# Block transposes that read with a stride, value rows in natural order, and fewer heads on VectorE at the border of two graphs

## The chip, the cores and the metric

The kernel runs on one core of one Trainium2 chip. The core has TensorE (PE: matmuls, and weight loads on a row of their own, PEld), VectorE (DVE), ScalarE (ACT), GpSimd (POOL) and SyncE (SP, which here only issues DMAs). They run at the same time and wait for each other through semaphores. The metric is the device time of one execution in microseconds (us); lower is better.

## The reference

There are 16 graphs of 1024 nodes with 256 features each, and an adjacency matrix per graph in which about one entry in 32 is set, the diagonal included. Two layers follow each other. Layer 0 normalizes the rows, applies a ReLU, and does masked attention with 8 heads of 32 features:

```python
h = jnp.maximum(_layernorm(x, axis=-1), 0.0)
Q, K, V = (proj(Wq, bq), proj(Wk, bk), proj(Wv, bv))          # per head
scores = jnp.einsum('bhnd,bhmd->bhnm', Q, K) * SCALE
scores = jnp.where(adj[:, None] == 0, -jnp.inf, scores)
attn = jax.nn.softmax(scores, axis=-1)
out = jnp.einsum('bhnm,bhmd->bhnd', attn, V)                  # heads joined
x = x + jnp.einsum('bno,po->bnp', out, Wo) + bo
```

Layer 1 normalizes again and attends once more, with one set of scores per kind of edge:

```python
h = jnp.maximum(_layernorm(x, axis=-1), 0.0)
e_k = leaky_relu(einsum('bid,bjd->bij', h * a_k[:, 0], h), 0.2)   # k = 0..3
scores = where(adj == k + 1, e_k, -9e15)
x = x + einsum('bij,bjd->bid', softmax(scores), h)
```

With the inputs given, entries of the adjacency are 0 or 1, so only the first kind occurs.

## The kernel before

**Tiles and steps.** A tile is 128 rows of one graph; a graph has 8 tiles, and 128 tiles are done in one loop (`for s in range(B * NT + 1)`), each with an inner loop over the 8 heads. Several pieces of work of different tiles run in one step of the loop: `now` is the tile whose layer 0 scores are made, `was` the one before it, whose heads are finished; `piece` and `piece_was` are rows of the next graph that are normalized and projected into queries, keys and values nine tiles ahead; `edge` and `edge_was` are tiles of layer 1, nine tiles behind. Each engine works in the order in which the loop issues; nothing reorders it. A tile's DMAs go on two queues, SP's and POOL's, and each is worked off in the order of its issues.

**A head.** TensorE makes a head's scores, 128x1024, in two matmuls (`scores`, L455) into one of two PSUM places, `sides[h in (4, 6)]`: heads 4 and 6, and layer 1's scores, use the second place, all others the first. VectorE adds the mask and takes the row minimum of the negated scores in one instruction (`softmax_max`, L467), which writes p to SBUF and so frees the PSUM place. ScalarE applies the exponential in place (`softmax_exp`, L475). Then p has to be turned, so that the 1024 keys lie on the partitions, and multiplied with the values (`combine`, L510; heads 0 to 3 at h = 7, heads 4 to 7 at h = 3 of the next tile).

**Two ways to turn.** For heads 2, 3, 6 and 7, TensorE makes eight 128x128 transposes and ScalarE copies them in two instructions (`turn`, `turn_half`, L574 and L575). For the heads in `BY_BLOCKS`, 0, 1, 4 and 5, VectorE transposes 32x32 blocks in one instruction (`blocks_of`, L376), and four DMAs on SP's queue place the four groups of partitions (`placed`, L381). The transpose reads p in one contiguous run. The keys therefore land on the partitions in another order within each 128: key 32b + k at partition 4k + b. The loop turns head h - 2 at head h, so head 5 of tile 7 is turned at h = 7 of that tile, and head 0 of tile 0 at h = 2 of that tile.

**Values.** Since two orders of keys exist, the values exist in two orders of rows: `values` (L339) makes columns 0 to 127 of v from `hTm`, whose rows are in the mixed order, and columns 128 to 255 from `hT`, in natural order. `place_of` tells where a head's 32 columns lie, the weight `wvT` and the bias `bv_t` have their columns in the same arrangement, and `combine` reads v at `place_of(h)`. The queries are made from `hTm` as well, so the tile's own rows are in mixed order in both layers. Layer 1 (`Edges`) uses `blocks_of` and `placed` too, on its own p, called sel.

**Keys.** A graph's eight keys are 512 KB loads from DRAM on SP's queue (`load_key`, L355). They replace the keys of the graph before in the same places, so they are issued at eight given steps (`KEY_STEPS`), four in tile 7 at h = 3, 4, 5 and 6, and four in tile 0 of the next graph at h = 0, 2, 3 and 4, between the block placements.

Of the kernel before, what the change touches and what calls it, by code (L numbers as in the profile page):

```python
# [17 lines left out]
P = 128  # L18
HEADS = 8
HD = 32  # L20
# [3 lines left out]
SLOPE = 0.2  # L24
NEG_INF = -9000000000000000.0
MASKED = -1e30
BY_BLOCKS = (0, 1, 4, 5)


def place_of(h):  # L30

    return (h // 2 % 2) * P + (h // 4) * 2 * HD + (h % 2) * HD


FLOOR = 1e28
# [7 lines left out]
def gnn_kernel(  # L43
# [18 lines left out]
    nc = tc.nc  # L62
    B, N, D = x.shape
    NT = N // P
    NC = D // P
    SCALE = HD ** (-0.5)
    HALF = 512
    NB = P // HD
# [35 lines left out]
    bv_t = const.tile([P, D], F32, name="bv_t")  # L104
    bo_t = const.tile([P, D], F32, name="bo_t")

    def load_biases():
        with nc.allow_non_contiguous_dma(reason="a few hundred elements, once"):
            nc.sync.dma_start(out=bq_t, in_=bq.rearrange("(c p) -> p c", p=P))
            nc.sync.dma_start(out=bk_t, in_=bk.rearrange("(c p) -> p c", p=P))  # L110
            for k, a in enumerate((a_0, a_1, a_2, a_3)):
                nc.sync.dma_start(out=a_t[:, :, k], in_=a.rearrange("(c p) o -> p (c o)", p=P))
        for i in range(2):
            nc.sync.dma_start(
                out=bv_t[:, i * P : (i + 1) * P].rearrange("p (r d) -> p r d", r=2),
                in_=bv.rearrange("(r i d) -> i r d", i=2, r=2)[i].partition_broadcast(P),
            )
        nc.sync.dma_start(out=bo_t, in_=bo.partition_broadcast(P))

    weight_rows = {}  # L120
# [6 lines left out]
    def transposed_weight(name):  # L127

        rows = weight_rows[name]
        wt = const.tile([P, NC, D], F32, name=name)  # L130
        tr = ps_tr.tile([P, 4, P], F32, tag="tr", name=f"{name}_tr")
        for fc in range(NC):
            for oc in range(NC):
                nc.tensor.transpose(tr[:, fc * NC + oc, :], rows[:, oc, fc * P : (fc + 1) * P], ident)
        if name == "wvT":
            for fc in range(NC):
                nc.vector.tensor_copy(
                    wt[:, fc].rearrange("p (i r d) -> p r i d", i=2, r=2),
                    tr[:, fc * NC : (fc + 1) * NC].rearrange("p r (i d) -> p r i d", i=2),
                )  # L140
        else:
            nc.vector.tensor_copy(wt.rearrange("p c f -> p (c f)"), tr.rearrange("p c f -> p (c f)"))
        return wt


    def norm_of(mv):

        g = nc.gpsimd
        n = mv.shape[1]

        def place(name, dtype=F32):
            if n <= 4:
                return small.tile([P, 4], dtype, tag=name, name=name)[:, :n]
            places.append(name)
            return many[:, len(places) * n - n : len(places) * n].bitcast(dtype)

        places = []
        if n > 4:
            many = work.tile([P, D], F32, tag="wide", name="many", bufs=1)

        ve = place("ve")
        g.tensor_scalar(ve, mv[:, :, 1], EPS, None, ALU.add)
        r = place("r")
        g.tensor_tensor(r, ve, less_half.to_broadcast([P, n]), ALU.pow)
        shift = place("shift")
        g.tensor_tensor(shift, mv[:, :, 0], r, ALU.mult)
        g.tensor_scalar(shift, shift, -1.0, None, ALU.mult)
        return r, shift
# [12 lines left out]
    qds, kds, vs, keysets, weights = {}, {}, {}, {}, {}  # L181

    class Piece:
# [146 lines left out]
        def values(self):  # L330
            b = self.b
            if b not in vs:
                vs[b] = graph.tile([P, NT, D], F32, tag="v", name=f"v_{b}")
            for t in range(self.n):
                ps = late if self.n == 1 else ps_tr.tile([P, D], F32, tag="tr", name="vproj")
                self.vproj = ps
                for i, hT in enumerate((self.hTm, self.hT)):
                    for fc in range(NC):
                        nc.tensor.matmul(  # L339
                            ps[:, i * P : (i + 1) * P],  # L340
                            lhsT=hT[:, fc, t * P : (t + 1) * P],
                            rhs=weights["wvT"][:, fc, i * P : (i + 1) * P],
                            start=(fc == 0),
                            stop=(fc == NC - 1),
                        )
                if self.n > 1:
                    self.biased(t)

# [25 lines left out]
    def blocks_of(p):  # L374
        blocks = work.tile([P, NB, NT, HD], F32, tag="blocks", bufs=3)
        nc.vector.transpose(blocks.rearrange("p b j q -> p j b q"), p)  # L376
        return blocks.rearrange("p b j q -> p b (j q)")
# [32 lines left out]
    class Attend:  # L410
# [69 lines left out]
            turn_half(self.probs[h][0], self.turned[h], half)  # L480

        def turn_blocks(self, h):
            self.blocks = blocks_of(self.probs[h][0])

        def place_blocks(self, h):
            self.turned[h] = placed(self.blocks, ptp.tile([P, N], F32, tag="pT", name="pT"))
# [19 lines left out]
        def combine(self, g):  # L506
            for j in range(NT):
                for r in range(GROUP):
                    h = g * GROUP + r
                    nc.tensor.matmul(  # L510
                        sums_place[r * HD : (r + 1) * HD, g * P : (g + 1) * P],
                        lhsT=vs[self.b][:, j, place_of(h) : place_of(h) + HD],
                        rhs=self.turned[h][:, j],
                        start=(j == 0),
                        stop=(j == NT - 1),
                    )
# [253 lines left out]
    with tc.manual_schedule():  # L770
# [6 lines left out]
        piece_was.load(nc.sync)  # L777
        now.load()
        load_biases()
        piece_next.load(nc.sync)  # L780
        mv = stats_place(NT)
# [3 lines left out]
        r, shift = norm_of(mv)  # L785
# [3 lines left out]
        for name in ("wkT", "wqT", "wvT", "woT"):  # L789
            weights[name] = transposed_weight(name)  # L790
# [28 lines left out]
        for s in range(B * NT + 1):  # L819
            b, t = divmod(s, NT)  # L820
# [8 lines left out]
            for h in range(HEADS):  # L829
                ending, eh = (now, h - 1) if h >= 1 else (was, HEADS - 1)  # L830
                turning, th = (now, h - 2) if h >= 2 else (was, HEADS + h - 2)
# [36 lines left out]
                if h == 3:  # L868
# [3 lines left out]
                        piece_was.biased()  # L872
                    if was:
                        was.combined()
                if turning and th in BY_BLOCKS:
                    turning.turn_blocks(th)
                    turning.place_blocks(th)
                elif turning:
                    turning.turn(th, 0)
                    turning.turn(th, 1)  # L880
# [162 lines left out]
```

## Time and profile before

| | us |
|---|---|
| runs: median (lowest to highest, three runs) | 3149.88 (3138.53 to 3151.07) |
| profiled execution: time | 3143.69 |
| its span, first to last instruction | 3141.9 |
| TensorE busy | 2941.3 (94%) |
| TensorE weight loads busy | 2202.9 (70%) |
| ScalarE busy | 2598.8 (83%) |
| VectorE busy | 2512.8 (80%) |
| POOL busy | 2172.4 (69%) |
| DMA packets of SP's queue, share of 16 engines | 54.5% |

The mean granted TensorE clock is 0.984 of full speed. VectorE does 520 block transposes of tiles called p (512 in layer 0 and 8 in the last graph's layer 1) and 120 of sel; both kinds take 1.24 us each. A line of groups reads: source line, engine, operation, out<-in by the program's names, partitions x elements and type, count, then busy us in all, mean ns of one, and after the last bar the idle time of the engine just before them with what ended it. In a timeline the first column is the start in us from the begin of the span, the second the length; in brackets stands the idle time before it. SPq is SP's queue of DMA issues. A window's row has, after the window, its length, the busy us of each engine with the number of instructions, the granted clock, the share of time that the DMA engines were busy, and GB/s.

### The profile page before, as it was taken

How to read it: one execution, taken by the hardware profiler on the slowest of the kernel's cores; microseconds unless marked ns; L12 is line 12 of the kernel's file. 1: busy time of each engine (PE TensorE's matmuls, PEld its weight loads, DVE VectorE, ACT ScalarE, POOL GpSimd, SP SyncE). 2: the span in 40 equal slices, each digit the busy share in tenths (PEclk: the TensorE clock that was granted, in tenths of full speed). 3: DMA queues.
4: the chain of work that ended last, by engine and by line, in shares of the span. 5: the costliest groups of instructions: out<-in, count | busy, mean ns of one | idle time of the engine just before them, and what ended most of it. 6: DMA issues, size and time to landing. Idle time of an engine off the chain costs nothing. (4 is left out here: it accounts for less than half of the span.)

```text
span 3141.9 us, 95789 instructions
## 1 busy us (share of the span) xinstructions
PE 2941.3 (94%) x36210; PEld 2202.9 (70%) x36210; DVE 2512.8 (80%) x4391; ACT 2598.8 (83%) x5157; POOL 2172.4 (69%) x2995
## 2 busy tenths in 40 slices
PE   5888999899999999999999999999999999998987
PEld 3666777677676777777777676777767777676663
DVE  4777888788787887878888787888878788787874
ACT  3888989889888988889889898888978888787871
POOL 2666777777777776777777777777767777675542
PEclk8999999999999999999999999999999999999999
DMA  6676787877878787787877878787787877777663
GB/s 214 208 245 212 230 272 220 270 217 230 255 229 263 223 263 225 226 268 223 270 227 235 251 234 257 228 258 229 234 261 215 271 223 227 245 232 239 185 174 96
DMA packets 634692, 729.22 MB, mean 232 GB/s; under 512 B 67376, under 2 KB 565424, under 8 KB 634224
## 3 DMA queue, kind: packets, MB, share of 16 engines
q1 hardware_dynamic: 565152, 510.86, 54.5%
q0 software_dynamic: 66960, 210.04, 20.5%
q8 instruction: 291, 4.77, 0.6%
q10 hardware_dynamic: 2112, 2.10, 0.2%
q14 instruction: 177, 1.45, 0.1%
HBM read 252.98 MB, written 134.22 MB: 123 GB/s over the span
## 5 line engine op out<-in xcount | busy, mean ns | idle before, releaser
L467 DVE CUSTOM_DVE_ANT_0 p<-s,neg 128x1024 f32<-128x1024 f32 x1024 | 1235.6, 1207 | 274.5 <-PE s L455 241.3
L475 ACT ACTIVATE p<-p,nmx 128x1024 f32<-128x1024 f32 x1024 | 1182.2, 1155 | 205.0 <-DVE nmx L467 202.5
L455 PE MATMUL s<-k,qt 128*128 128x512 f32 x2048 | 764.9, 455 | 107.9 <-DMA k<-kd 72.5
L376 DVE STREAM_TRANSPOSE blocks<-p 128x1024 f32<-128x1024 f32 x520 | 643.7, 1238 | 20.5 <-ACT p L663 10.6
L575 ACT COPY pT<-trp 128x512 f32<-128x512 f32 x1024 | 547.0, 590 | 106.2 <-PE trp L574 106.2
L510 PE MATMUL acc<-pT,v 128*32 128x128 f32 x16384 | 559.0, 281 | 37.1 <-DMA pT<-blocks 22.1
L510 PEld LDWEIGHTS acc<-pT,v 128*32 128x32 f32 x16384 | 472.6, 113 | 156.5 <-issue 82.9
L574 PE MATMUL trp<-ident,p 128*128 128x128 f32 x4096 | 531.2, 273 | 1.6 <-ACT pT L575 1.5
L574 PEld LDWEIGHTS trp<-ident,p 128*128 128x128 f32 x4096 | 478.1, 140 | 73.2 <-ACT pT L575 3.1
L435 POOL TENSOR_SCALAR neg<-adj 128x1024 bf16<-128x1024 int32 x128 | 467.6, 3653 | 79.5 <-ACT neg L447 70.2
L681 PE MATMUL acc<-h,pT 128*32 128x256 f32 x8192 | 494.7, 383 | 8.8 <-DVE ot L690 8.8
L455 PEld LDWEIGHTS s<-k,qt 128*128 128x128 f32 x2048 | 324.3, 192 | 215.5 <-issue 79.5
L681 PEld LDWEIGHTS acc<-h,pT 128*32 128x32 f32 x8192 | 241.8, 110 | 211.9 <-issue 63.8
L659 POOL TENSOR_TENSOR sel<-sel,less 128x1024 f32<-128x1024 f32 x120 | 286.6, 2388 | 64.9 <-ACT less L648 44.9
L616 PE MATMUL s<-h1T,ha 128*128 128x512 f32 (+2 forms) x744 | 272.8, 490 | 2.6 <-ACT h1T L553 1.3
L657 POOL TENSOR_SCALAR less<-top 128x1 f32<-128x1 f32 x120 | 31.6, 264 | 274.5 <-DVE top L639 274.5
L319 POOL DMA_DIRECT2D qd<-halves x240 | 177.0, 777 | 58.7 <-POOL halves L309 31.8
L494 POOL COPY wide<-rec 128x256 f32<-128x256 f32 x128 | 53.9, 421 | 226.5 <-DVE rec L492 226.5
L475 ACT ACTIVATION_READ_ACCUMULATOR p<-p,nmx 128x1 f32 x1024 | 202.7, 198 | 0.0
L325 POOL DMA_DIRECT2D kd<-halves x240 | 171.7, 764 | 35.4 <-POOL halves L309 35.4
L309 POOL TENSOR_TENSOR halves<-full,halves 128x256 fp32r<-128x256 f32 x240 | 176.3, 735 | 20.6
L648 ACT ACTIVATE less<-sel 128x1024 f32<-128x1024 f32 x120 | 127.0, 1058 | 65.6 <-DVE top L639 65.6
(120 smaller groups left out, 4238.8 us busy)
## 6 DMA issues: line engine op xcount, KB each, us to landing
pT<-blocks SPq DMA_DIRECT2D x2560, 128.0 KB, 3.6
k<-kd SPq DMA_DIRECT2D x128, 512.0 KB, 6.1
qt<-qd SPq DMA_DIRECT2D x128, 512.0 KB, 4.4
adj<-in_adj POOLq DMA_DIRECT2D x127, 512.0 KB, 5.1
qd<-halves POOLq DMA_DIRECT2D x240, 256.0 KB, 3.0
kd<-halves POOLq DMA_DIRECT2D x240, 128.0 KB, 4.0
xb<-in_x POOLq DMA_DIRECT2D x128, 128.0 KB, 4.4
x1d<-x SPq DMA_DIRECT2D x128, 128.0 KB, 4.0
```

Source lines behind the costliest of these rows:

```text
L319: nc.gpsimd.dma_start(out=qds[self.b][self.first, oc].rearrange("p u w n -> p u (w n)"), in_=halves.unsqueeze(1).to_broadcast([P, 2, 2 * P]),)
L376: nc.vector.transpose(blocks.rearrange("p b j q -> p j b q"), p)
L435: nc.gpsimd.tensor_scalar(self.neg, self.adj, 0.0, MASKED, ALU.is_equal, ALU.mult)
L455: nc.tensor.matmul(self.ps[:, cols], lhsT=self.qt[:, h, :], rhs=keysets[self.b][h][:, cols], start=True, stop=True,)
L467: nc.vector.tensor_tensor_reduce(out=p, in0=sides[h in (4, 6)], in1=self.neg, scale=-SCALE, scalar=FLOOR, op0=ALU.add, op1=ALU.min, accum_ ...
L475: nc.scalar.activation(p, p, AF.Exp, bias=nmx, scale=-1.0, accum_out=self.sums[:, h : h + 1])
L510: nc.tensor.matmul(sums_place[r * HD : (r + 1) * HD, g * P : (g + 1) * P], lhsT=vs[self.b][:, j, place_of(h) : place_of(h) + HD], rhs=self ...
L574: nc.tensor.transpose(tr[:, j, :], p[:, jj * P : (jj + 1) * P], ident)
L575: copy(pT[:, half * 4 : half * 4 + 4, :], tr)
L616: nc.tensor.matmul(self.side[:, cols], lhsT=self.ha[:, c, :], rhs=h1T[:, c, cols], start=(c == 0), stop=(c == NC - 1),)
L659: nc.gpsimd.tensor_tensor(self.sel, self.sel, self.less, ALU.subtract)
L681: nc.tensor.matmul(sums_place[a * HD : (a + 1) * HD, :], lhsT=self.pT[:, j, a], rhs=h1s[self.b][:, j, :], start=(j == 0), stop=(j == NT - 1),)
```

## The change

Values are kept in natural row order for all heads. The block transposes of layer 0 read p through a view that takes every fourth element, 32 of them, then the next offset, so that the natural order comes out on the partitions; the elements of one run of the read are 16 bytes apart. What the transpose writes and the four placing DMAs are the same. `values` then needs only `hT`, and makes all 256 columns in one pair of matmuls; `place_of` and the special arrangements of `wvT` and `bv_t` go. `hTm` stays, for the queries. Layer 1's own block transposes are not touched. As all heads read the same v, the set of heads that VectorE turns may differ by tile: it is 0, 1, 4 in tile 7, 1, 4, 5 in tile 0, and 0, 1, 4, 5 in the others.

```diff
-BY_BLOCKS = (0, 1, 4, 5)
-
-
-def place_of(h):
-
-    return (h // 2 % 2) * P + (h // 4) * 2 * HD + (h % 2) * HD
+BY_BLOCKS = {7: (0, 1, 4), 0: (1, 4, 5)}
+
+
+def by_blocks(t):
+    return BY_BLOCKS.get(t, (0, 1, 4, 5))
...
-        for i in range(2):
-            nc.sync.dma_start(
-                out=bv_t[:, i * P : (i + 1) * P].rearrange("p (r d) -> p r d", r=2),
-                in_=bv.rearrange("(r i d) -> i r d", i=2, r=2)[i].partition_broadcast(P),
-            )
+        nc.sync.dma_start(out=bv_t, in_=bv.partition_broadcast(P))
...
-        if name == "wvT":
-            for fc in range(NC):
-                nc.vector.tensor_copy(
-                    wt[:, fc].rearrange("p (i r d) -> p r i d", i=2, r=2),
-                    tr[:, fc * NC : (fc + 1) * NC].rearrange("p r (i d) -> p r i d", i=2),
-                )
-        else:
-            nc.vector.tensor_copy(wt.rearrange("p c f -> p (c f)"), tr.rearrange("p c f -> p (c f)"))
+        nc.vector.tensor_copy(wt.rearrange("p c f -> p (c f)"), tr.rearrange("p c f -> p (c f)"))
...
-                for i, hT in enumerate((self.hTm, self.hT)):
-                    for fc in range(NC):
-                        nc.tensor.matmul(
-                            ps[:, i * P : (i + 1) * P],
-                            lhsT=hT[:, fc, t * P : (t + 1) * P],
-                            rhs=weights["wvT"][:, fc, i * P : (i + 1) * P],
-                            start=(fc == 0),
-                            stop=(fc == NC - 1),
-                        )
+                for fc in range(NC):
+                    nc.tensor.matmul(
+                        ps,
+                        lhsT=self.hT[:, fc, t * P : (t + 1) * P],
+                        rhs=weights["wvT"][:, fc, :],
+                        start=(fc == 0),
+                        stop=(fc == NC - 1),
+                    )
...
-            self.blocks = blocks_of(self.probs[h][0])
+            self.blocks = blocks_of(self.probs[h][0].rearrange("p (j k b) -> p j b k", b=NB, k=HD))
...
-                        lhsT=vs[self.b][:, j, place_of(h) : place_of(h) + HD],
+                        lhsT=vs[self.b][:, j, h * HD : (h + 1) * HD],
...
-                if turning and th in BY_BLOCKS:
+                if turning and th in by_blocks(turning.t):
```

## The prediction

> **What bounds the kernel now.** I read first the page's busy shares, then the windows of single tiles, then the timeline of TensorE and VectorE where one tile passes into the next, then the groups of instructions for prices. The page names TensorE:
>
> ```profile
> PE 2941.3 (94%) x36210; PEld 2202.9 (70%) x36210; DVE 2512.8 (80%) x4391; ACT 2598.8 (83%) x5157; POOL 2172.4 (69%) x2995
> L376 DVE STREAM_TRANSPOSE blocks<-p 128x1024 f32<-128x1024 f32 x520 | 643.7, 1238 | 20.5 <-ACT p L663 10.6 <-DMA pT<-blocks 5.4 <-issue 2.5
> ```
>
> 94% is a mean over two kinds of tile. A tile is the time from one score reduction of head 0 (L467) to the next tile's. By their starts in the trace, tiles 1 to 6 of graphs 1 to 15 take 22.4 to 23.6 us on the mean of their place, 22.8 together; tile 7 takes 22.3; tile 0 takes 29.4. Tile 4 of graph 2 and tile 0 of graph 3 in the windows view (first column the window, then busy us by engine):
>
> ```profile
> 510.31:533.01 22.70, 22.65 (x287) 17.14 (x286) 19.45 (x34) 20.42 (x40) 18.82 (x29) 1.00 0.79 236
> 600.15:631.05 30.90, 23.57 (x287) 17.80 (x286) 19.64 (x34) 19.97 (x39) 20.59 (x29) 0.94 0.95 315
> ```
>
> In the ordinary tile TensorE is busy 22.65 of 22.70 us, and VectorE has 3.25 us to spare. In tile 0 both idle, and the DMA engines are at 0.95: TensorE waits for the next graph's keys, and its combine (L510) lasts 2.91 us where 1.95 is usual:
>
> ```profile
> 610.12 1.19 PE L455 MATMUL s<-k,qt 128*128 128x512 f32 x2 [3.62 <-DMA k<-kd]
> 611.24 2.91 PE L510 MATMUL acc<-pT,v 128*32 128x128 f32 x64
> ...
> 617.38 0.73 PE L455 MATMUL s<-k,qt 128*128 128x512 f32 x2 [0.83 <-DMA k<-kd]
> ...
> 627.67 0.70 PE L455 MATMUL s<-k,qt 128*128 128x512 f32 x2 [2.68 <-DMA k<-kd]
> ```
>
> VectorE's spare time is not spread evenly. At the seam between two ordinary tiles its timeline is
>
> ```profile
> 529.30 1.24 DVE L376 STREAM_TRANSPOSE blocks<-p 128x1024 f32<-128x1024 f32 x1
> 530.46 1.19 DVE L467 CUSTOM_DVE_ANT_0 p<-s,neg 128x1024 f32<-128x1024 f32 x1
> 531.58 0.08 DVE L467 DVE_READ_ACCUMULATOR2_ANT nmx<- 128x1 f32 x1
> 531.58 1.24 DVE L376 STREAM_TRANSPOSE blocks<-p 128x1024 f32<-128x1024 f32 x1
> 533.01 1.23 DVE L467 CUSTOM_DVE_ANT_0 p<-s,neg 128x1024 f32<-128x1024 f32 x1 [0.19 <-POOL shift L167]
> ```
>
> and TensorE's
>
> ```profile
> 532.15 0.73 PE L455 MATMUL s<-k,qt 128*128 128x512 f32 x2
> 532.72 1.04 PE L574 MATMUL trp<-ident,p 128*128 128x128 f32 x8
> 533.59 0.60 PE L610 MATMUL s<-ident,mirror 128*128 128x128 f32 x4
> 534.30 0.73 PE L455 MATMUL s<-k,qt 128*128 128x512 f32 x2
> ```
>
> Heads 0 and 1 share one PSUM place for scores, so TensorE's scores of head 1 (534.30) may start only when VectorE has reduced head 0 (533.01 + 1.23 = 534.24). That leaves 0.06 us of slack on TensorE and 0.19 us of idle on VectorE, behind the transposes of heads 4 and 5.
>
> **The change, part by part.** The sum is made against the profiled execution, 3143.7 us (span 3141.9), 6 us under the median of the runs, 3149.9.
>
> *v in natural order.* The value projection goes from eight TensorE instructions of 128 columns to four of 256. By the timeline the eight (L339) run from 516.33 until L500 starts at 517.22, 0.89 us. The output projection (L525) is the new form, four of 128x256: 521.84 until the next scores at 522.51, 0.67 us. So 0.22 us less in each of the 120 tiles that project, on TensorE where it is the bound. The eight projections of the start give 2 us, with one bias load and one weight copy fewer or simpler.
>
> *Fewer heads on VectorE in tiles 7 and 0.* 32 heads (5 of each tile 7, 0 of each tile 0) lose a 1.24 us block transpose and four SP DMAs of some 0.6 us of issue each, and gain eight TensorE transposes (532.72 to 533.59: 0.87 us) and two ScalarE copies (2 x 0.59 us; ScalarE idles over 2 us in every tile). Tile 7 is TensorE-bound: 0.87 - 0.22 = +0.65 us, 16 times, +10. In tile 0 the eight DMAs stand on SP ahead of the key loads:
>
> ```profile
> 602.26 5.46 SPq L381 DMA_DIRECT2D pT<-blocks  x4
> ...
> 611.95 4.12 SPq L381 DMA_DIRECT2D pT<-blocks  x4
> ```
>
> Those are head 5 of tile 7 and head 0 of tile 0. Landings of such DMAs on the full queue follow each other by some 0.33 us, so what stands behind all eight comes 8 x 0.33 = 2.6 us earlier: the last key, whose wait is 2.68 us, and the combine's excess of 0.96 us goes with head 5. The 3.62 us wait is for a key queued ahead of them; it stays, and hides head 0's 0.87 us on TensorE. I take 2.6 of at most 2.68 + 0.83 + 0.96 = 4.5 us, and at least 0 if the landing is set by POOL's transfers, which share the engines. With v, 2.8 us less in each of 15 tile 0s.
>
> *The read with a stride.* 480 block transposes remain (512 less 32), each reading 1024 elements of p 16 bytes apart. No row shows VectorE reading SBUF so. It can't be a gain: the elements are as many. Low end 0: VectorE's copy from PSUM with a 128-byte step (L237) takes 690 ns, contiguous ones of that size (L142) 658 to 692. High end: the only engine row that reads SBUF with a step is POOL's:
>
> ```profile
> L596 POOL TENSOR_SCALAR ha<-h1T,a_t 128x128 f32<-128x128 f32 x248 | 149.4, 725 | 4.0 <-PE s L616 3.2
> L659 POOL TENSOR_TENSOR sel<-sel,less 128x1024 f32<-128x1024 f32 x120 | 286.6, 2388 | 64.9 <-ACT less L648 44.9 <-DMA pT<-blocks 20.0
> ```
>
> L596 less the 225 ns of a two-element TENSOR_SCALAR (L162) is 4.0 ns an element with a 128-byte step. Contiguous, L659 against the 735 ns of 256 elements (L309) gives 2.15. If VectorE paid those 1.82 ns more, a transpose would take 1.86 us more. I take the ratio instead, 1.84, since the memory is the same but the engine is not: VectorE's contiguous slope is (690 - 420)/256 = 1.05 ns (L142 and L137 copies), so 0.84 x 1.05 x 1024 = 0.9 us more, 2.1 us a transpose. I prefer it to the PSUM row because the step is paid where the memory is read, and this is SBUF.
>
> What it costs: at the seam two transposes grow, heads 4 and 5, with only 0.19 + 0.06 us ahead of the next TensorE instruction: 2 x 0.9 - 0.25 = 1.55 us in which TensorE waits. Heads 0 and 1 lie amid VectorE idles (0.67, 0.19, 0.51 us around them, and 0.64 ahead of head 4); I cost them at nothing, and beyond about 1 us each that cover is gone. VectorE would be busy 19.4 + 3.6 = 23.0 us of about 24.1, so it just fits. Behind a longer transpose on VectorE's queue stand the next reductions, and ScalarE's exponentials wait for those.
>
> [...]
>
> *Sum at 0.9 us:* tiles 1 to 6: 1.55 x 96 - 0.22 x 90 (the last graph projects nothing) = +129, or 1.3 a tile. Tile 7: +10. Tile 0: -2.8 x 15 = -42, but head 5 at its end still grows the seam by 0.9 - 0.25 = 0.65 us (head 4 is hidden in the last key's wait): +10. Start: -2. Together +105: 3143.7 + 105 = about 3249 us.
>
> **The rivals.**
>
> *The stride is free.* For it: the PSUM rows, and ScalarE's write to SBUF with a 16-byte step (L245, 381 ns against 375 contiguous, L244). Against it: L596. Then tiles 1 to 6 give -0.22 x 90 = -20, tile 7 +10, tile 0 -42, start -2: -54, so 3090 us, faster. By the sum, a growth of s us costs (2s - 0.25) x 96 + (s - 0.25) x 15 against 54 us saved, so no change lies at s = 0.40 us, a transpose of 1.63 us; below it the kernel gains.
>
> *VectorE becomes the bound everywhere.* [...] At the high end, 1.86 us, 27.3 us a tile: +432 (0.4 idle left or less) and some 30 in tile 7, 3600 us. For it: L596's absolute price. Against it: POOL is slow at contiguous rows too.
>
> *Tile 0 keeps its waits.* POOL's transfers hold the keys back as before: the forecast loses 2.6 x 15 = 39 us, 3288.
>
> **How the numbers follow.** The stride free or nearly so: 0.27 (faster). Around the break-even: 0.03. The forecast with s from 0.45 to 1.2 us, with or without tile 0's gain: 0.58; its own range is 3155 to 3340. VectorE the bound: 0.12. Half a per cent, 16 us, is about what a measurement of this kernel can tell from no change. The range must reach to the free stride, 3090 less 15, and up to 3400, within the VectorE-bound case, which leaves about 0.1 above.
>
> **What would show it.** After the change the block transposes of p should read near 2.1 us, those of sel (unchanged) 1.24. VectorE's busy share should rise to about 90% and TensorE's fall to about 91%; TensorE's scores should wait for L467's successor at the seam, by 1.5 us a tile. L525's price for the value projection should show as four instructions in 0.67 us, and tile 0 should shorten by 2 us while tiles 1 to 6 lengthen by 1.3. I am wrong if the transposes of p stay at 1.24 us.

## The result

The changed kernel takes 3335.8 us (median of four runs), the kernel before 3144.2 us beside it: a ratio of 1.063, 95% interval 1.057 to 1.069. The forecast, 3249 us, lies between them; the direction was right and the loss, 192 us, is 1.8 times the 105 us that the sum gave. The profiled execution took 3334.0 us, its span 3332.2.

The page of the changed kernel, its busy shares and the group of block transposes:

```profile
PE 2989.5 (90%) x35954; PEld 2195.4 (66%) x35954; DVE 2860.9 (86%) x4358; ACT 2629.0 (79%) x5221; POOL 2173.2 (65%) x2995
L363 DVE STREAM_TRANSPOSE blocks<-p 128x1024 f32<-128x1024 f32 x488 | 1014.0, 2078 | 11.1 <-ACT p L650 10.6
```

Eight of the 488 transposes are layer 1's, contiguous; without them a strided one takes 2.09 us, 0.85 more than before. TensorE has fallen from 94% to 90%: it now waits. The groups of score matmuls and of their weight loads by shape say for whom (columns as before; at the end idle time and what ended it):

```profile
L442 PE MATMUL s<-k,qt 128*128 128x512 f32 x2048 | 762.6, 454 | 266.7 <-DVE nmx L454 117.1 <-DMA k<-kd 65.5 <-ACT mirror L617 56.5
L442 PEld LDWEIGHTS s<-k,qt 128*128 128x128 f32 x2048 | 322.9, 193 | 400.8 <-DVE nmx L454 188.5 <-ACT mirror L617 84.9 <-issue 76.3
```

The same group of matmuls before:

```profile
L455 PE MATMUL s<-k,qt 128*128 128x512 f32 x2048 | 764.9, 455 | 107.9 <-DMA k<-kd 72.5 <-DMA qt<-qd 15.5 <-DVE nmx L467 11.6
```

TensorE's waits ahead of its scores were 72.5 us for keys and 11.6 us for VectorE's reduction. The wait for keys is nearly as long as it was, the one for the reduction is ten times as long, and ScalarE's mirror copy, which held no score matmul up before, has 56.5 us of its own. In the timeline of tile 4 of graph 2, the tile whose window the prediction shows, first VectorE at the seam where it begins and then TensorE:

```profile
543.36 2.10 DVE L363 STREAM_TRANSPOSE blocks<-p 128x1024 f32<-128x1024 f32 x1
545.36 1.22 DVE L454 CUSTOM_DVE_ANT_0 p<-s,neg 128x1024 f32<-128x1024 f32 x1
```

```profile
543.52 0.73 PE L442 MATMUL s<-k,qt 128*128 128x512 f32 x2 [0.37 <-DVE nmx L454]
...
546.65 0.73 PE L442 MATMUL s<-k,qt 128*128 128x512 f32 x2 [0.75 <-DVE nmx L454]
...
555.83 0.73 PE L442 MATMUL s<-k,qt 128*128 128x512 f32 x2 [0.58 <-ACT mirror L617]
```

The first two waits are the seam that the prediction named: 0.37 + 0.75 = 1.12 us, where it gave 1.55 (at the end of the same tile they are 0.37 and 1.08). The third, 0.58 us ahead of head 4's scores, it costed at nothing. ScalarE's timeline shows where that one comes from:

```profile
554.25 1.06 ACT L635 ACTIVATE less<-sel 128x1024 f32<-128x1024 f32 x1 [1.21 <-DVE top L626]
555.21 0.57 ACT L617 COPY mirror<-s 128x512 f32<-128x512 f32 x1
```

Head 0's longer transpose stands on VectorE ahead of layer 1's reduction (L626); ScalarE waits 1.21 us for that, does its part of the leaky ReLU (`less`, called bend below), and only then copies the mirror blocks out of the second PSUM place; head 4's scores need that place.

Lengths of tiles, from the starts of head 0's reduction in each profile, means over graphs 1 to 15, in us; all kernels of the study but e4 in one table. Each ratio is to runs of the kernel before that were made beside the run:

| kernel | tile 0 | tiles 1 to 6 | tile 7 | median, us | ratio to before (95%) |
|---|---|---|---|---|---|
| before | 29.4 | 22.8 | 22.3 | 3144.2 | |
| changed | 28.8 | 24.6 | 23.6 | 3335.8 | 1.063 (1.057 to 1.069) |
| e1, contiguous read | 26.8 | 22.8 | 23.2 | 3115.8 | 0.992 (0.989 to 0.994) |
| e2, uniform sets | 29.4 | 24.6 | 24.2 | 3357.8 | 1.068 (1.063 to 1.073) |
| e3, exponential permutes | 26.4 | 23.7 | 24.1 | 3238.3 | 1.031 (1.026 to 1.036) |
| e5, stride for heads 4, 5 | 27.3 | 23.9 | 22.9 | 3227.9 | 1.025 (1.021 to 1.029) |
| e6, stride for heads 0, 1 | 28.2 | 23.4 | 23.8 | 3225.6 | 1.026 (1.022 to 1.030) |
| e7, changed, keys early | 24.8 | 24.5 | 23.6 | 3262.6 | 1.037 (1.034 to 1.041) |
| e8, before, keys early | 26.9 | 22.8 | 22.2 | 3106.5 | 0.988 (0.984 to 0.992) |
| e9, before, one pair for v | 29.2 | 22.7 | 22.4 | 3139.4 | 0.998 (0.996 to 1.000) |
| e10, before, keys earlier | 27.8 | 22.8 | 22.3 | 3120.6 | 0.991 (0.988 to 0.994) |
| e11, e1 with keys early | 23.5 | 22.8 | 23.3 | 3061.7 | 0.972 (0.970 to 0.975) |
| e12, sets without stride | 23.2 | 22.7 | 23.2 | 3061.3 | 0.974 (0.971 to 0.977) |

### The profile page after: what moved, and what is told of

The parts are those of the page before. It is cut to its first block, busy times and chain, and to the rows that moved or that the text cites. A ratio compares the mean times of both kernels' runs of the same rounds, so it can differ in the third digit from the quotient of the medians.

```text
span 3332.2 us, 94986 instructions
## 1 busy us (share of the span) xinstructions
PE 2989.5 (90%) x35954; PEld 2195.4 (66%) x35954; DVE 2860.9 (86%) x4358; ACT 2629.0 (79%) x5221; POOL 2173.2 (65%) x2995
## 5 line engine op out<-in xcount | busy, mean ns | idle before, releaser
L363 DVE STREAM_TRANSPOSE blocks<-p 128x1024 f32<-128x1024 f32 x488 | 1014.0, 2078 | 11.1 <-ACT p L650 10.6
L562 ACT COPY pT<-trp 128x512 f32<-128x512 f32 x1088 | 582.5, 591 | 60.5 <-PE trp L561 60.1
L561 PE MATMUL trp<-ident,p 128*128 128x128 f32 x4352 | 573.0, 275 | 1.9 <-ACT pT L562 1.8
L497 PE MATMUL acc<-pT,v 128*32 128x128 f32 x16384 | 548.3, 282 | 15.5 <-ACT recT L491 14.4
L561 PEld LDWEIGHTS trp<-ident,p 128*128 128x128 f32 x4352 | 498.9, 141 | 95.3 <-ACT pT L562 28.0
```

The source lines that it names most:

```text
L497: nc.tensor.matmul(sums_place[r * HD : (r + 1) * HD, g * P : (g + 1) * P], lhsT=vs[self.b][:, j, h * HD : (h + 1) * HD], rhs=self.turned[h ...
L561: nc.tensor.transpose(tr[:, j, :], p[:, jj * P : (jj + 1) * P], ident)
L562: copy(pT[:, half * 4 : half * 4 + 4, :], tr)
```

## The experiments

### e1: is the stride the whole loss?

```diff
-            self.blocks = blocks_of(self.probs[h][0].rearrange("p (j k b) -> p j b k", b=NB, k=HD))
+            self.blocks = blocks_of(self.probs[h][0])
```

> The changed kernel, but the block transposes of layer 0 read p in one contiguous run again, while v stays in natural order: the products of heads 0, 1, 4 and 5 pair keys with wrong rows of v, so those heads' outputs are wrong; the work is otherwise the same. If the stride is the whole loss, block transposes of p are back at 1.24 us and the time falls below the kernel before, to about 3090 us (3144 less 20 for v, less 42 in tile 0, plus 10 in tile 7). If natural v or the uneven sets of heads cost something of their own, it stays above 3144 us.

3115.8 us, below the kernel before. The stride costs 3335.8 - 3115.8 = 220 us; all else in the change gains 26 to 28 us, where 54 were expected. The table says where: tile 0 gains 2.6 us (expected 2.8), tile 7 loses 0.9 (expected 0.65), but tiles 1 to 6 gain nothing, where v was to bring 0.22 us each. Tile 4 of graph 3 in the two kernels, TensorE's timeline (start, length), before and then e1:

```profile
706.59 0.61 PE L339 MATMUL acc<-wvT,hTm 128*128 128x128 f32 x4
707.04 0.61 PE L339 MATMUL acc<-wvT,hT 128*128 128x128 f32 x4
707.48 0.38 PE L500 MATMUL acc<-ident,wide 128*128 128x128 f32 x2
```

```profile
708.07 1.03 PE L326 MATMUL acc<-wvT,hT 128*128 128x256 f32 x4
708.93 0.38 PE L487 MATMUL acc<-ident,wide 128*128 128x128 f32 x2
```

From the start of the value projection to the next instruction it is 0.89 us before and 0.86 in e1. In the trace the single starts stand 111 ns apart at 128 columns and 216 ns apart at 256, so eight come to 0.89 us and four to 0.86. The weight loads are half as many in e1, 190 ns each where they took 192, but they stood beside the matmuls before: in the tile shown the first starts at 706.17 us and the other seven run from 706.60 to 707.46, the matmuls from 706.59 to 707.65. The prediction's 0.67 us was read off the output projection, whose last instruction is followed by a score matmul that starts 28 ns after it and whose partner starts later in turn, 425 ns after it.

### e9: the value projection by itself

```diff
-                for i, hT in enumerate((self.hTm, self.hT)):
-                    for fc in range(NC):
-                        nc.tensor.matmul(
-                            ps[:, i * P : (i + 1) * P],
-                            lhsT=hT[:, fc, t * P : (t + 1) * P],
-                            rhs=weights["wvT"][:, fc, i * P : (i + 1) * P],
+                for fc in range(NC):
+                    nc.tensor.matmul(
+                        ps,
+                        lhsT=self.hT[:, fc, t * P : (t + 1) * P],
+                        rhs=weights["wvT"][:, fc, :],
```

> The kernel before, but the value projection makes all 256 columns from the rows in natural order in one pair of matmuls; heads 0, 1, 4 and 5 then meet values in the wrong order, so that their outputs are wrong and the rest of the work is the same. The prediction's price, 0.22 us a tile on TensorE: 3142 less 28 gives 3115 us. The price read off the instructions' starts in the contiguous variant, four times 216 ns against eight times 111 ns, 0.03 us a tile: 3140 us, no change.

3139.4 us, a ratio of 0.998 (0.996 to 1.000): 0.03 us a tile or nothing. Natural v, then, is no gain on TensorE that these runs can tell from nothing; what e1 gains is the uneven sets' work.

### e2: the uneven sets

```diff
-BY_BLOCKS = {7: (0, 1, 4), 0: (1, 4, 5)}
+BY_BLOCKS = {}
```

> The changed kernel with VectorE turning heads 0, 1, 4 and 5 in every tile. If the sets relieve the border of two graphs, tile 7 and tile 0 together lengthen by 2 to 3 us per graph and the time is 3365 to 3385 us. If the extra transposes on TensorE cost what they save elsewhere, it is 3336 us within 10.

3357.8 us, 22 us more than the changed kernel, somewhat less than expected: tile 0 lengthens by 0.6 and tile 7 by 0.6 us. The sets do relieve the border of two graphs, by 1.2 us a graph under the stride and, by e1's table row (-2.6 and +0.9 against before), by 1.7 without it.

### e4: what a step costs

Fourteen forms, four times each, behind the end of the kernel before; `plain` and `quads` are the views of 128x1024 floats with the inner run contiguous and with steps of four elements, `spaced(x, n)` has steps of n. The last multiplication, L1026, reads runs of two adjacent floats, each run 32 bytes behind the one before.

```diff
+            nc.vector.transpose(plain(to), plain(src))                      # L1016
+            nc.vector.transpose(plain(to), quads(src))                      # L1017
+            nc.vector.transpose(quads(to), plain(src))                      # L1018
+            nc.vector.transpose(whole(to, 2), spaced(src, 2))               # L1019
+            nc.vector.transpose(whole(to, 8), spaced(src, 8))               # L1020
+            nc.vector.transpose(whole(to, 32), spaced(src, 32))             # L1021
+            nc.vector.tensor_scalar(plain(to), plain(src), 2.0, None, ALU.mult)   # L1022
+            nc.vector.tensor_scalar(plain(to), quads(src), 2.0, None, ALU.mult)   # L1023
...
+            nc.vector.tensor_scalar(whole(to, 2), spaced(src, 2), 2.0, None, ALU.mult)   # L1025
...
+            nc.scalar.activation(plain(to), plain(src), AF.Exp)             # L1031
+            nc.scalar.activation(plain(to), quads(src), AF.Exp)             # L1032
+            nc.scalar.activation(quads(to), plain(src), AF.Exp)             # L1033
```

> The kernel before with single instructions added behind its end, to read prices off: block transposes, multiplications by a constant and exponentials of 128x1024 floats, reading or writing with different steps. The 16-byte read should cost a transpose 2.09 us as in the changed kernel. If the price is paid per 8-byte pair of words, an 8-byte step costs as much as a 16-byte one and runs of two adjacent words cost nothing more than contiguous ones; if it is paid per 16-byte line, an 8-byte step costs nothing. If it belongs to the transpose and not to the read, the multiplication keeps its contiguous time.

The groups by shape of this run (after the bar: busy us, mean ns of one):

```profile
L1032 ACT ACTIVATE to<-src 128x1024 f32<-128x1024 f32 x4 | 8.1, 2012 | 0.1
L1020 DVE STREAM_TRANSPOSE to<-src 128x1024 f32<-128x1024 f32 x4 | 8.0, 2006 | 0.1
L1033 ACT ACTIVATE to<-src 128x1024 f32<-128x1024 f32 x4 | 8.0, 1998 | 0.1
L1017 DVE STREAM_TRANSPOSE to<-src 128x1024 f32<-128x1024 f32 x4 | 7.9, 1981 | 0.1
L1018 DVE STREAM_TRANSPOSE to<-src 128x1024 f32<-128x1024 f32 x4 | 7.9, 1978 | 0.1
L1021 DVE STREAM_TRANSPOSE to<-src 128x1024 f32<-128x1024 f32 x4 | 7.6, 1904 | 0.1
L1016 DVE STREAM_TRANSPOSE to<-src 128x1024 f32<-128x1024 f32 x4 | 5.0, 1245 | 2.4 <-DVEq L1041 2.3
L1019 DVE STREAM_TRANSPOSE to<-src 128x1024 f32<-128x1024 f32 x4 | 5.0, 1245 | 0.1
...
L1023 DVE TENSOR_SCALAR to<-src 128x1024 f32<-128x1024 f32 x4 | 4.3, 1070 | 0.1
L1031 ACT ACTIVATE to<-src 128x1024 f32<-128x1024 f32 x4 | 4.2, 1056 | 78.4 <-DVE to L1026 78.3
L1025 DVE TENSOR_SCALAR to<-src 128x1024 f32<-128x1024 f32 x4 | 2.8, 694 | 0.1
L1026 DVE TENSOR_SCALAR to<-src 128x1024 f32<-128x1024 f32 x4 | 2.8, 694 | 0.1
L1022 DVE TENSOR_SCALAR to<-src 128x1024 f32<-128x1024 f32 x4 | 2.8, 694 | 0.1
```

On VectorE, reading with a step of 8 bytes is free (L1019 and L1025: 1245 ns and 694 ns, as contiguous), and so, for the multiplication, are runs of two adjacent words with a hop between them (L1026: 694 ns). A step of 16 bytes costs the transpose 0.74 us (1981 ns), and 32 or 128 bytes cost much the same (2006 and 1904 ns). It is paid on the write (L1018: 1978 ns) as on the read (L1017), by the multiplication (L1023: +0.38 us on a base of 0.69) and by ScalarE (+0.96 us for the read, L1032, +0.94 for the write, L1033, on a base of 1.06). So it is neither the transpose's nor VectorE's alone. All tiles here lie in SBUF; the copies of the kernel before that step by 128 bytes in PSUM show none of it (VectorE's L237, 690 ns beside the 658 to 692 of L142; ScalarE's L245, 381 beside the 375 of L244). The free step of 8 bytes speaks against the first of the expected cases, a price for each pair of words. No write with a step of 8 bytes was tried, and on ScalarE no step of 8 bytes at all. Inside the kernel, beside the other engines, the strided transpose takes 2.09 us instead of 1.98; why is open.

### e3: let ScalarE do the permuting

```diff
         def softmax_exp(self, h):
...
+            if h in by_blocks(self.t):
+                e = work.tile([P, N], F32, tag="p", name="e", bufs=4)
+                nc.scalar.activation(
+                    e.rearrange("p (j b k) -> p j k b", b=NB, k=HD), p.rearrange("p (j k b) -> p j k b", b=NB, k=HD),
+                    AF.Exp, bias=nmx, scale=-1.0, accum_out=self.sums[:, h : h + 1],
+                )
+                self.probs[h] = (e, nmx)
```

and the transpose reads it contiguously.

> The changed kernel, but ScalarE's exponential of the heads that VectorE turns reads p in steps of four elements and writes another tile in block order, so that the transpose reads one contiguous run and the result is right. If ScalarE reads with a 16-byte step at full rate, its exponential stays at 1.16 us, the transposes are at 1.24 us and the time is about 3090 us, better than both kernels. If ScalarE pays for the step as VectorE does (some 0.85 ns an element, 0.87 us for each of four heads), ScalarE has 20.3 + 3.5 = 23.8 us of work a tile and the time is 3250 to 3350 us.

3238.3 us. The first idea fell: ScalarE pays for the step as well, and the loss is somewhat less than the second range had it. As the edit is written, the read of p runs on and it is the write of e that steps, by 32 floats or 128 bytes. Its groups by line:

```profile
L464 ACT ACTIVATE e<-p,nmx 128x1024 f32<-128x1024 f32 x480 | 1040.1, 2167 | 5.7 <-DVE nmx L454 5.7
...
L470 ACT ACTIVATE p<-p,nmx 128x1024 f32<-128x1024 f32 x544 | 643.4, 1183 | 57.8 <-DVE nmx L454 57.7
L363 DVE STREAM_TRANSPOSE blocks<-e 128x1024 f32<-128x1024 f32 x480 | 594.0, 1238 | 0.8
```

2167 against 1183 ns, with the transposes back at 1238. In tiles 3 to 6 ScalarE has 0.04 to 0.26 us of idle left (medians over the graphs): it has become the bound, and the price, 0.98 us four times a tile, went from an engine with 3.3 us to spare to one with 2.3. That it loses less than the changed kernel, +96 against +192 us, although the single price is higher, fits that the place of a longer instruction counts and not its length alone.

### e5 and e6: which transposes cost?

```diff
+            p = self.probs[h][0]
+            if h in (4, 5):
+                p = p.rearrange("p (j k b) -> p j b k", b=NB, k=HD)
-            self.blocks = blocks_of(self.probs[h][0].rearrange("p (j k b) -> p j b k", b=NB, k=HD))
+            self.blocks = blocks_of(p)
```

and the same with `(0, 1)`.

> The changed kernel with the strided read for heads 4 and 5 alone; heads 0 and 1 read p in one run, so that their outputs are wrong and the work is the same. Theory 1, the prediction's: the loss is made at the border of two tiles, where two longer transposes stand ahead of head 0's reduction; nearly all of the 1.9 us that tiles 1 to 6 lose against the contiguous read stays, 1.4 to 1.9 us a tile, and the time is 3255 to 3320 us. Theory 2, the loss is VectorE's total of work: half of it stays, 0.9 us a tile, 3215 to 3235 us.

> The changed kernel with the strided read for heads 0 and 1 alone; heads 4 and 5 read p in one run, so that their outputs are wrong and the work is the same. Theory 1 as the prediction had it: idle time of VectorE takes these two in, 3116 to 3130 us. Theory 1 as the trace of the changed kernel corrects it: head 0's longer transpose pushes layer 1's reduction, ScalarE's mirror copy after it and so the scores of head 4, 0.6 us a tile, and head 1's holds the last key's load in tile 0, some 1 us there: 3180 to 3200 us. Theory 2, VectorE's total: 0.9 us a tile, 3215 to 3235 us.

3227.9 and 3225.6 us: against e1, +112 and +110, together the 220 of the full stride. Both lie outside the ranges of theory 1; by the totals this is theory 2, half for each pair. The tiles and the waits say otherwise. In tiles 1 to 6 heads 4 and 5 cost 1.1 us and heads 0 and 1 cost 0.55 us; with both strided it is 1.8. Heads 0 and 1 make up for it elsewhere: tile 0 +1.4 us, tile 7 +0.5, and graph 0, whose eight tiles run without layer 1, +19.3 us in all against +10.3 from heads 4 and 5. Each pair makes its own wait. The chain of waiting engines, first e5 and then e6 (engine and line, whom it waited for, us in all, times, longest):

```profile
PE s L442 <- DVE nmx L454: 123.3, 198, 1.6
...
PEld s L442 <- ACT mirror L620: 15.0, 73, 0.4
```

```profile
PEld s L442 <- ACT mirror L620: 74.4, 102, 1.2
...
PE s L442 <- ACT mirror L620: 46.6, 94, 0.9
...
PE s L442 <- DVE nmx L454: 10.7, 26, 1.4
```

With the stride on heads 4 and 5 TensorE waits 123.3 us for the reduction, as in the changed kernel, and its matmuls hardly for the mirror copy; with heads 0 and 1 it waits 46.6 us for the mirror copy and 10.7 for the reduction, e1's 10.9. So the prediction's mechanism holds for heads 4 and 5 (1.1 us where 2 x 0.85 - 0.25 = 1.45 was its formula), and in tiles 1 to 6 a second chain, which it did not have, runs from heads 0 and 1 through ScalarE. Graph 0 needs a third, as the mirror copy is layer 1's: there TensorE waits 8.2 us for loads of queries in e6 and 0.7 in e1, and these loads stand on SP's queue right behind block placements, which wait for the transposes. The rest of graph 0's 19.3 us was not taken apart. Nor is VectorE the bound by its total: in the changed kernel's tiles 2 to 6 it still idles 1.8 to 2.0 us.

### e7 and e8: why does tile 0 keep its wait?

Of the 2.6 us that tile 0 was to gain, the changed kernel shows 0.6. Its queue of SP and TensorE's timeline in tile 0 of graph 3:

```profile
648.94 1.28 SPq L342 DMA_DIRECT2D k<-kd  x2
656.35 3.22 SPq L368 DMA_DIRECT2D pT<-blocks  x4
659.67 0.53 SPq L409 DMA_DIRECT2D qt<-qd  x1
660.25 0.73 SPq L342 DMA_DIRECT2D k<-kd  x1
```

```profile
650.76 0.70 PE L442 MATMUL s<-k,qt 128*128 128x512 f32 x2 [1.14 <-DMA k<-kd]
...
667.29 1.19 PE L442 MATMUL s<-k,qt 128*128 128x512 f32 x2 [4.54 <-DMA k<-kd]
```

SP issues nothing from 650.22 to 656.35: the next entry places head 1, whose transpose VectorE has not made yet, and the last key's load stands behind it. It is issued at 660.25, and head 7's scores start at 667.29.

```diff
-    KEY_STEPS = (6, 9, 10, 13, 16, 20, 22, 24)
+    KEY_STEPS = (6, 9, 10, 13, 16, 20, 21, 22)
```

> The changed kernel with the last two key loads of a graph issued two and one slots earlier, ahead of head 1's placement in tile 0. If the last key is late because its issue stands on SP's queue behind the four DMAs that wait for head 1's transpose, the 2 to 4.5 us wait ahead of head 7's scores in tile 0 goes, tile 0 shortens by 2 to 3.5 us and the time is 3285 to 3310 us. If the landing is set by how full the DMA engines are, the wait stays and the time is 3336 us within 10.

> The kernel before with the same two key loads issued earlier. Its last key costs 1.2 to 3.7 us of wait in tile 0; if that is the place on SP's queue, the time is 3110 to 3125 us; if the DMA engines are full there anyway, no change, 3142 us within 10.

In the changed kernel 73 us less (3262.6), more than expected: TensorE's wait for keys falls from 65.5 to 14.5 us, and tile 0 from 28.8 to 24.8 us. The kernel before takes 3106.5 us with them, beside 3148.6 without, ratio 0.988 (0.984 to 0.992), a little more than expected too. Tile 0 of graph 3 in the windows view, the changed kernel and then e7:

```profile
642.42:672.06 29.64, 23.85 (x291) 18.38 (x290) 20.82 (x33) 20.87 (x41) 20.00 (x28) 0.94 0.84 283
636.43:660.63 24.20, 23.42 (x298) 18.00 (x297) 20.79 (x33) 21.44 (x43) 18.77 (x27) 1.00 0.91 317
```

The place on the queue was the cause, not how full the DMA engines were: they are busy 0.84 of the time with the wait and 0.91 without it. The granted clock, 0.94 against 1.00, shows why the gain is larger than the wait alone. In the changed kernel it falls to half at 666.9 us, during the wait, and stays there for 3.4 us; the score pair behind the wait takes 1.19 us, where 0.70 is usual. In tile 0 of graphs 1 to 15 the clock is at half for 5.2 us on the mean in the changed kernel (in 13 of the 15) and for 0.5 us in e7 (in one). The clock's share, estimated as half of that difference, is up to 2.4 of the 4.0 us that tile 0 gains.

### e10: all key loads earlier

```diff
-    KEY_STEPS = (6, 9, 10, 13, 16, 20, 22, 24)
+    KEY_STEPS = (6, 8, 10, 11, 13, 16, 18, 20)
```

> The kernel before with the key loads at steps 6, 8, 10, 11, 13, 16, 18 and 20. If the wait for key 3 in tile 0, 1.2 to 3 us, also comes from its place on SP's queue (behind head 4's placement and the store of layer 0's rows), tile 0 gains another 1 to 2 us against the two moved loads, 3075 to 3090 us. If the DMA engines are full there, the waits move to other placements and it stays at 3106 us within 10.

3120.6 us, 14 more than with two loads moved and outside both ranges: tile 0 is 27.8 us instead of 26.9. The trace shows where the waits went:

```profile
L455 PE MATMUL s<-k,qt 128*128 128x512 f32 x2048 | 766.0, 455 | 37.1 <-DMA qt<-qd 16.7 <-DVE nmx L467 12.4 <-DMA k<-kd 0.7
L510 PE MATMUL acc<-pT,v 128*32 128x128 f32 x16384 | 565.9, 284 | 83.1 <-DMA pT<-blocks 64.7 <-ACT recT L504 17.9
```

TensorE no longer waits for keys, 0.7 us instead of 42.0 in e8, but ahead of its combine it waits 64.7 us for block placements, where it was 22.4 in e8. The effect is that of the second theory, waits that move to other placements, though the time is longer than it said.

### e11 and e12: sets and early keys, without the stride

e11 is e1 with e7's key steps.

> The changed kernel with the contiguous read (heads 0, 1, 4 and 5 have wrong outputs, the work is otherwise the same) and the last two key loads moved earlier. If the uneven sets and the earlier loads relieve the same queue, most of the 26 us that the sets brought is contained in the 36 us of the earlier loads: 3095 to 3110 us. If they add, 3075 to 3085 us.

3061.7 us, ratio 0.972 (0.970 to 0.975). The two gains more than add, which neither theory had: 0.8% (e1) and 1.2% (e8) alone, 2.8% together. Tile 0 is at 23.5 us, less than 1 us over the others; with either change alone it was at 26.8 or 26.9. The granted clock is part of it: in tile 0 it is at half for 4.3 us on the mean before, for 3.0 in e1, 3.2 in e8 and 0.5 in e11.

e12 keeps values in two orders and the contiguous read, as before, and takes the uneven sets and the early keys. Heads 5 of tile 7 and 0 of tile 0 need their 32 columns in natural order; these are copied. Of the edit, the copies:

```diff
...
+    def rows_in_order(b, h):
+        place = const.tile([P, NT, HD], F32, name=f"v_rows{h}") if h not in in_rows else in_rows[h]
+        in_rows[h] = place
+        for r in range(NB):
+            nc.gpsimd.dma_start(
+                out=place[r * HD : (r + 1) * HD], in_=vs[b][r::NB, :, place_of(h) : place_of(h) + HD]
+            )
...
-                        lhsT=vs[self.b][:, j, place_of(h) : place_of(h) + HD],
+                        lhsT=in_rows[h][:, j]
+                        if h in (0, 1, 4, 5) and h not in by_blocks(self.t)
+                        else vs[self.b][:, j, place_of(h) : place_of(h) + HD],
...
+                if h == 6 and t == NT - 1 and b + 1 < B:
+                    rows_in_order(b + 1, 0)
+                if h == 6 and t == 3 and b < B:
+                    rows_in_order(b, 5)
```

> A version with right results meant to be faster than both: the kernel before (values in two orders, contiguous reads), with the uneven sets of heads and the two key loads moved earlier. Where heads 5 of tile 7 and 0 of tile 0 go through TensorE they need their values in natural order; four small DMAs a graph and head on POOL's queue make that copy of 32 columns ahead of time. To make room, the buffers for the halves of queries and keys go from two to one. If the copies and the lost buffer are hidden, it comes near the contiguous variant with early keys, 3060 to 3080 us. If POOL's queue delays the loads of tile 0, what the sets brought is lost: 3095 to 3115 us.

3061.3 us, ratio 0.974 (0.971 to 0.977): faster than both kernels, and level with e11. The copies take 128 issues of 0.59 us on POOL, and no tile but 0 and 7 changes. This is what the uneven sets and the earlier keys bring together without the strided read.

## Why the prediction came out as it did

The changed kernel lies inside the range given for the forecast, 3155 to 3340 us, by 4 us. The price was right, and the wait at the seam was in kind. The terms that were put at nothing or too well, heads 0 and 1 and the value projection, come to more than the 85 us that the sum lacked, and the seam, which was put too high, gives part of it back; so that the time stayed inside the range is in part luck.

**The price of a strided transpose: right.** 0.9 us more was taken, 0.85 measured. The way to it, the ratio of POOL's rows, was luck in part: it was 1.84, and in e4 the whole times of a 16-byte read stand to the contiguous ones as 1.59 for the transpose, 1.54 for the multiplication and 1.91 for ScalarE. The rows that spoke for a free step had PSUM on one side. ScalarE's copy from PSUM to `hTm` (L245), 381 against 375 ns, was among them, and it was misread as a write with a 16-byte step. By its two views in the kernel it writes `hTm` in one run and reads PSUM in steps of 32 floats, so no step falls on SBUF; between two places in SBUF a 16-byte step costs ScalarE 0.94 to 0.96 us for 1024 elements (e4).

**The seam behind heads 4 and 5: right in its mechanism, too large.** 1.55 us was predicted, 1.12 us shows at one seam in the timeline and 1.1 us a tile in e5.

**"Heads 0 and 1 lie amid VectorE idles ... I cost them at nothing": wrong.** This step failed, and e6 shows it: 110 us. The idle times were VectorE's, and what mattered was who waits for the instruction behind the transpose. Layer 1's reduction stands right behind head 0's transpose; ScalarE's bend and mirror copy, and with them the second PSUM place, hang on it. In tiles 1 to 6 that is 0.55 us, 50 us in all. By e6's profile the rest is 21 us in tile 0, through SP's queue (e7), 19 us in graph 0, in part through that queue too, and 8 us in tile 7.

**"0.22 us less in each of the 120 tiles": wrong, mis-read.** The value projection saves 0.03 us (e1, e9). With it some 20 us of the sum are gone.

**Tile 0: -32 us predicted with its part of the seam, about -9 measured.** The queue relief came out at the size given, -2.6 us a tile without the stride (e1), but by luck: its parts were others. By the traces, on the mean of tile 0 in graphs 1 to 15, the last key's wait, which was to go, is 2.4 us in e1 and was 2.2 before. What fell is the wait for head 3's key, which was to stay, from 2.1 to 0.8 us, and the combine of heads 4 to 7 from 4.2 to 2.1. Nor does the combine of 2.91 us show a late head 5: the granted clock of the kernel before is at half from 609.7 to 613.1 us, from the end of the 3.62 us wait on, and covers most of it. With the stride, the step that failed is that the longer transposes would touch tile 0 only at its end: head 1's holds SP's queue, and the last key behind it (e7), and the clock falls in that wait.

**Tile 7: +10 predicted, about +18 measured** (23.6 against 22.3 us over graphs 1 to 14, and 21.2 against 21.7 in graph 0).

Graph 0 adds its own: its eight tiles, 20.5 us each before, take 22.5 us, +16 us together, where the general 1.3 us was put in for six of them. Put together, tiles 1 to 6 of graphs 1 to 15 give (24.63 - 22.79) x 90 = 166 us, tile 7 +18, tile 0 -9 and graph 0 +16: 191 us, beside the measured difference of the spans, 3332.2 - 3141.9 = 190.3.

**The rivals.** The free stride is excluded by the 2.09 us. VectorE as the bound everywhere did not come about at this price. Of "tile 0 keeps its waits" the effect was right, its cause (POOL's transfers) was not.

## What to carry to other kernels

Before an instruction is made longer "inside idle time", ask of the next instruction on its engine who waits for it, and follow that for one more engine; the idle time of the engine itself says little. Look at the inner step of a read or a write of floats in SBUF: here a read on VectorE with 8 bytes cost nothing (1245 and 694 ns, as contiguous, e4), while the passes with 16 bytes and more, reads and writes, cost 0.4 to 1 us more per 1024 elements, on VectorE (e4) and on ScalarE (e3, e4). And look at what stands on a queue behind a DMA that waits for a late producer: here SP issued nothing for 6.1 us (650.22 to 656.35), and the last key's load stood behind that DMA (e7). So issue the loads that could go early ahead of such a DMA, but not so early that they hold up the placements in their turn (e10: 64.7 us of waits for them, 22.4 in e8). And look at the granted clock behind a wait of TensorE: by the estimate in e7 it is up to 2.4 of the 4.0 us that tile 0 gains there.

## What was not expected of the hardware

A float read with a step of 8 bytes was free for VectorE's transpose and one of 16 bytes cost it 59%, after which 32 and 128 bytes cost much the same (1245, 1981, 2006, 1904 ns). ScalarE paid at least as much as VectorE, 0.96 us for 1024 elements in a read and 0.94 in a write, beside 0.74 and 0.73 for the transpose. Halving the number of weight loads of a projection saved 0.03 us of 0.89: four instructions of 256 columns stand 216 ns apart, eight of 128 columns 111 ns apart. And with the key waits of tile 0 the granted clock falls to half there: for 5.2 us a tile in the changed kernel, 0.5 with the two loads moved (e7).
